# Attention with interleaved encoder work: stages handed out by a model of the engines' times, and the softmax sums' round trip through DRAM timed in microseconds

## The chip, the cores and the metric

The kernel runs on one core of a Trainium2 chip. The metric is device time in microseconds (us) for one execution; lower is better. The engines are TensorE (PE in the profile; PEld are its weight loads), VectorE (DVE), ScalarE (ACT), GpSimd (POOL) and SyncE (SP, which here only issues DMAs). Each takes its own instructions in the order in which the program was written.

## The reference

`x` has the shape (4, 1024, 256), that is B = 4 sequences of T = 1024 tokens with C = 256 channels. Two layers are added to it in turn.

```
def attn(x):                       # H = 16 heads of D = 16 channels
    q, k, v = split(x @ w_attn.T)
    att = q @ k.T / sqrt(16) + where(causal, slope[h] * (kpos - qpos), -inf)
    return (softmax(att) @ v) @ w_proj.T

def ffn(x):                        # attention over the 4 sequences, at each position
    q, k, v = split(x @ in_proj_w.T + in_proj_b)
    h = layernorm(x + softmax(q @ k.T / 4) @ v @ out_w.T + out_b)
    assign = max(top_2(softmax(h @ router_w.T + router_b)))   # one of 8 experts
    oe = gelu(h @ w1[assign].T + b1[assign]) @ w2[assign].T + b2[assign]
    return layernorm(h + oe)

x = x + attn(layernorm(x))
x = x + ffn(layernorm(x))
```

All of it is in float32. Attention is causal within a sequence of 1024 tokens. The second layer's attention mixes the four tokens that share a position, and each token then goes to one expert.

## The kernel before

**Attention.** The work is cut into 20 *units* (line 676 on). A unit is a batch `n`, that is a chunk `c` of 256 query tokens of a sequence `b`. In the last chunk the 256 tokens are split, so there are 8 units of 128 tokens (`size` 1); the others have `size` 2. For a unit and a group `g` of four heads, keys are taken in *rounds* of 512 columns: `score` (L951) makes the scores of a round on PE, 4 heads side by side in the rows, into two pairs of PSUM banks, ACT takes the exponentials, and `weigh` (L988) multiplies two rounds' results by the values. There are 160 rounds, that is 80 pairs `p`. `begins[u]` is the pair at which unit `u` starts; its last rounds are weighed one pair after its end.

The scores are transposed (keys on partitions), so the softmax sum of each query comes out as one more row of `yt`, next to 16 rows of each head. To divide, that row has to reach the partitions of its head. It goes through DRAM, all on SyncE's queue:

| step | what it issues |
| --- | --- |
| end of `weigh` | `y<-yt`: the unit's result to DRAM |
| `load_sums` (L1039) | `sums<-y`: the sums, spread over 128 partitions |
| `invert` (L1045) | DVE reciprocal, then `r<-inverse` to DRAM |
| `load_y` (L1053) | two times `su<-r` (each inverse repeated for 16 channels) and `yc<-y` |
| `divide` (L1070) | DVE: `yc` times `su` |
| `project` (L1079) | PE: `op<-wp,yc`; DVE adds it to `x` |

The last unit, 19, goes another way (`normalise`, `project_slots`).

**Preparing a batch.** For each `n` there are `x_norm` in three stages (L850), `turn` (L862), two `project_qk` (L875) and `value` (L897). `fill_slots` (L921) loads a group's queries and keys into `slots`, on SyncE, once the previous unit's last score of that group is out.

**Encoder fronts.** `front` (L1547) is a generator: the second layer's part ahead of the experts for 128 positions (512 tokens). It needs `x` after `project` of all four sequences. There are 8 fronts, 0 to 7. Front 7 is done after attention, with the first expert tiles; the others are spread through attention. At each `yield` a front says of which kind its next stage is, and its cost in us: "E" and "P" are work of DVE (P follows a result of another engine), "N" an exponential on ACT, "R" a power on POOL, "D" and "d" products on PE (d: a further one of the same kind), "DQ" the start of the projection to `qkv`, whose one buffer only one front can hold. A class `Running` keeps the next stage; at most two fronts are under way.

**Who decides the order.** Each pair `p` is written out as: `score_next(2p)`, `E_slot(2p)`, `D_slot(p)`, `fill()`, `take_E`, `score_next(2p+1)`, `weigh` of the two oldest rounds, `fill()`, `E_slot(2p+1)`. Steps with a fixed place are put in with `at_E(slot, ...)` and `at_D(pair, ...)`; the sums' steps stand at E slots `2e+3`, `2e+5`, `2e+6` and `2e+9` and at D slot `e+5`, with `e = begins[u+1]`, and the fronts of a chunk join the queue at E slot `2e+11`. The rest of a slot goes to the fronts: `take_E` (L2021) moves each front by at most one E, N, R or P stage, up to 2.5 us of cost in a slot (`E_SLOT`; 3.6 in the last chunk, `E_LATE`), and `take_D` (L2038) hands out D stages up to 5.6 us in a pair (`D_SLOT`), not in the slot in which the front's previous stage went out.

**After attention.** A second planner (L2293) places what is left of the fronts, front 7 and the expert tiles of the first six fronts; the remaining tiles follow when front 7's routing is known. An expert tile gathers 128 tokens of one expert (POOL), runs two products and a layer norm, and scatters its rows (POOL).

Of the kernel before, what the change touches and what calls it, by code (L numbers as in the profile page):

```python
# [37 lines left out]
P = 128  # L38
B, T, C = 4, 1024, 256
H, D, E = 16, 16, 8  # L40
S = 32
G = H // 4
# [5 lines left out]
PC = W // P  # L48
NC = T // W
# [20 lines left out]
TILE = (("PE", 2.6), ("DVE", 1.7), ("ACT", 1.9), ("POOL", 2.3))  # L70
TILE_HALF, LAG, COPIED, FIRST_BY, W1_THERE, LOAD_W2 = 1.3, 0.2, 1.0, 0.1, 22.0, 10.0
KQ_BUFS = 2
D_SLOT, E_SLOT, E_LATE = 5.6, 2.5, 3.6

EXP_ZERO = -126 * math.log(2.0)

# [526 lines left out]
def fast_layer(ctx: ExitStack, tc: tile.TileContext, odd, x, wq, wk, wv, wp, w_in, w_out, w_r,  # L603
# [32 lines left out]
    fact = ctx.enter_context(pool("fact", 1))  # L636
# [15 lines left out]

    half_of, n_pairs = [], [0]
    tail_banks = []

    def pair_of_banks(name):
        half_of.clear()
        n_pairs[0] += 1  # L660
        return ps_s.tile([P, 2, QC], F32, tag=f"s{n_pairs[0] % 4}", name=name)

    def bank(name):
# [9 lines left out]
    batches = [(c, b) for c in range(NC) for b in range(B)]  # L673


    units = [(n, 0, PC if n < (NC - 1) * B else 1) for n in range(NC * B)]
    units += [(n, i, 1) for i in range(1, PC) for n in range((NC - 1) * B, NC * B)]
    last_unit = len(units) - 1
# [23 lines left out]
    for j in range(4):  # L702
        r = j * S + D
# [99 lines left out]
    def norm_stats(src, n, name, tag=""):  # L803
        tiles = norm_tiles(name, tag)
        for i in range(n):
            norm_one(tiles, i, src(i))
        return norm_end(tiles, n)

    def norm_root(rstd, n):
        nc.gpsimd.tensor_tensor(  # L810
            rstd[:, :n], rstd[:, :n], minus_half.to_broadcast([P, n]), ALU.pow
        )
# [30 lines left out]
    sums, at = [], 0  # L843
# [6 lines left out]
    def x_norm(n, stage):  # L850
        c, b = batches[n]
        src = lambda i: xs[c, b][:, i]
        if stage == 0:
            held["norm", n] = norm_stats(src, PC, f"x_{n}", "_x")
        elif stage == 1:
            norm_root(held["norm", n][1], PC)
        else:
            xn = act.tile([P, PC, C], F32, tag="xn", name=f"xn_{n}")
            norm_apply(lambda i: xn[:, i], src, PC, *held.pop(("norm", n)), f"x_{n}")
            held["xn", n] = xn  # L860
# [76 lines left out]
    def blocks_of(u, r):  # L937

        n, i, size = units[u]
        first = batches[n][0] * PC + i  # L940
        some = QC // (size * P)
        return [
            (kb, max(0, kb - first) * P)
            for kb in range(some * r, min(some * (r + 1), first + size))
        ]

    def n_rounds(u):
        n, i, size = units[u]
        return -(-(batches[n][0] * PC + i + size) // (QC // (size * P)))
# [129 lines left out]
    def project(u):  # L1079
        yc, _ = held.pop(("y", u))  # L1080
        pm = bank(f"op_{u}")
        for i in range(units[u][2]):
            for cc in range(CC):
                nc.tensor.matmul(
                    pm[:, i * C:(i + 1) * C], yc[:, cc, i * P:(i + 1) * P], wp_sb[:, cc],
                    start=cc == 0, stop=cc == CC - 1,
                )
        add_attended(u, pm)
# [4 lines left out]
    for j in range(4):  # L1093
        at = slice(j * S, (j + 1) * S)
# [901 lines left out]

    class Running:
        def __init__(self, stages):
            self.stages, self.slot, self.was, self.ready = stages, -9, None, 0.0
            self.next()  # L2000

        def next(self):
# [2 lines left out]
                self.kind, self.cost, *self.more = self.kind  # L2005

    queue, running = [], []
    slot = [0]
    to_load, left_x = [], [0] * NC

    def load_next():
        while to_load and (
            to_load[0] < X_BUFS or left_x[(to_load[0] - X_BUFS) // B] == PC
        ):
            load_x(to_load.pop(0))

    def start_fronts():
        while queue and len(running) < 2:
            running.append(Running(queue.pop(0)))

    def take_E(cost=0.0, most=E_SLOT):  # L2021


        slot[0] += 1
        start_fronts()
        for it in list(running) if most > 0 else ():
            if it.kind in ("E", "N", "R", "P") and it.slot < slot[0] - (it.kind == "P"):
                of_it = it.cost if it.kind in ("E", "P") else 0.0
                if cost and cost + of_it > most:
                    continue  # L2030
                cost += of_it
                it.slot, it.was = slot[0], "E"
                it.next()
                if it.kind == "end":
                    running.remove(it)
        return cost

    def take_D(cost):  # L2038

        slot[0] += 1  # L2040
        for it in list(running):
            while it.kind[0] in "Dd":
                if it.kind == "DQ" and ("qkv",) in held:
                    break
                if it.kind != "d" or it.slot < slot[0]:
                    if it.slot >= slot[0] - (it.was == "E"):
                        break
                if cost and cost + it.cost > D_SLOT:
                    break
                if it.kind == "DQ":  # L2050
                    held["qkv",] = True
                cost += it.cost
                it.slot, it.was = slot[0], "D"
                it.next()
            if it.kind == "end":
                running.remove(it)
        return cost

    begins = [0]
    for u in range(len(units)):  # L2060
        begins.append(begins[-1] + G * n_rounds(u) // 2)
    of_E, of_D = {}, {}

    def at_E(k, what):
        of_E.setdefault(k, []).append(what)

    def at_D(k, cost, what):
        of_D.setdefault(k, []).append((cost, what))
# [4 lines left out]
    for u, (n, i, size) in enumerate(units):  # L2073
        c, b = batches[n]

        q = begins[u - 1] if u else -2
        e = begins[u + 1]
        if u == n:
            if n > 2:
                at_E(2 * begins[n - 3], lambda n=n: to_load.append(n))  # L2080
            for k in range(3):
                at_E(2 * q - 7 + k, lambda n=n, k=k: x_norm(n, k))
            at_D(q - 2, 0.9, lambda n=n: turn(n))

            at_D(q - (n == 0), 1.7, lambda n=n: project_qk(n, 0))
            at_D(q + (n > 0), 1.7, lambda n=n: project_qk(n, 1))
            at_D(q + 2, 1.7, lambda n=n: value(n))
        if u > 1:
            at_E(2 * q + 1, lambda u=u: load_values(u))
        if u < last_unit:  # L2090
            for at, what in ((3, load_sums), (5, invert), (6, load_y), (9, divide)):
                at_E(2 * e + at, lambda u=u, what=what: what(u))
            at_D(e + 5, 0.9 * size, lambda u=u: project(u))
        if b == B - 1 and u < last_unit:
            at_E(2 * e + 11, lambda c=c, i=i, size=size: queue.extend(
                front(PC * c + i + k, fact, 1, False) for k in range(size)
            ))
    at_E(2 * begins[last_unit] + 1, load_slotted)
    for g in range(2):
        at_D(begins[last_unit] + 2 + g, 0.5, lambda g=g: normalise(g))  # L2100
# [36 lines left out]

    fetching = [True]

    def E_slot(k, most=E_SLOT):  # L2140
        for what in of_E.pop(k, ()):
            what()
        load_next()
        if tables and fetching:
            experts.fetch()
        return take_E(0.0, most)

    def D_slot(p):
        todo = of_D.pop(p, ())
        for _, what in todo:  # L2150
            what()
        return take_D(sum(cost for cost, _ in todo))

    for p in range(-6, 0):
        E_slot(2 * p)
# [3 lines left out]
    rounds = [  # L2159
        (u, g, r) for u in range(len(units)) for g in range(G) for r in range(n_rounds(u))  # L2160
    ]
    waiting, to_fill = [], []

    def score_next(k):
        u, g, r = rounds[k]
        waiting.append((u, g, r, score(u, g, r)))
        if r == n_rounds(u) - 1 and u < last_unit:
            to_fill.append((u + 1, g))

    def fill():  # L2170
        while to_fill:
            fill_slots(*to_fill.pop(0))

    for p in range(len(rounds) // 2):
        most = E_SLOT if p < begins[(NC - 1) * B] else E_LATE

        then = most if p < len(rounds) // 2 - 1 else 0.0
        score_next(2 * p)
        E_slot(2 * p, most)
        D_slot(p)  # L2180
        fill()
        take_E(0.0, then)
        score_next(2 * p + 1)
        if len(waiting) > 2:
            weigh(waiting[:2])
            del waiting[:2]
        fill()
        E_slot(2 * p + 1, then)
    weigh(waiting)
    attention.close()  # L2190
    half_of.clear()
    tail_banks.append(ctx.enter_context(pool("ps_m", 3, space=PSUM)))


    for p in range(len(rounds) // 2, len(rounds) // 2 + 3):
        for k in (2 * p, 2 * p + 1):
            for what in of_E.pop(k, ()):
                what()
            if k % 2 == 0:
                for _, what in of_D.pop(p, ()):  # L2200
                    what()
    assert not of_E and not of_D, (sorted(of_E), sorted(of_D))
    for g in range(2, G):
        normalise(g)
    load_sums(last_unit)
# [87 lines left out]
    while threads:  # L2293
# [4 lines left out]
        at, _, it = min((begin(it) + FIRST_BY * n, n, it) for n, it in enumerate(threads))  # L2298
# [14 lines left out]
    n = 0  # L2313
# [98 lines left out]
```

## Time and profile before

| what | value |
| --- | --- |
| median of 3 runs | 840.61 us (839.70 to 841.50) |
| the profiled execution | 839.0 us; span of its instructions 837.3 us |
| granted clock of TensorE, mean | 0.945 |
| 38 to 107 us: first chunk, no fronts | PE busy 59.2 of 69 |
| 107 to 657 us: rest of attention with fronts 0 to 6 | PE 500.8, DVE 369.9, ACT 308.4 of 550 |
| 657 to 740 us: front 7 and tiles | PE 72.1, DVE 69.5 of 83 |
| 740 to 838 us: tiles | PE 67.2, POOL 69.3, DVE 59.1 of 98 |

The stretches come from a view of busy time by window. A line of the profile names an instruction by what it writes and reads, `yc<-yc,su` for the division. Nearly all instructions carry line 584, a helper that records every operation, so that names of tiles tell them apart. In a line of the timeline the numbers are start and length; a bracket holds the idle time of the engine just before, and what ended it. In a line of the waits they are total, number and longest.

### The profile page before, as it was taken

How to read it: one execution, taken by the hardware profiler on the slowest of the kernel's cores; microseconds unless marked ns; L12 is line 12 of the kernel's file. 1: busy time of each engine (PE TensorE's matmuls, PEld its weight loads, DVE VectorE, ACT ScalarE, POOL GpSimd, SP SyncE). 2: the span in 40 equal slices, each digit the busy share in tenths (PEclk: the TensorE clock that was granted, in tenths of full speed). 3: DMA queues.
4: the chain of work that ended last, by engine and by line, in shares of the span. 5: the costliest groups of instructions: out<-in, count | busy, mean ns of one | idle time of the engine just before them, and what ended most of it. 6: DMA issues, size and time to landing. Idle time of an engine off the chain costs nothing. (4 is left out here: it accounts for less than half of the span.)

```text
span 837.3 us, 22499 instructions
## 1 busy us (share of the span) xinstructions
PE 721.3 (86%) x8917; PEld 538.9 (64%) x8917; DVE 546.5 (65%) x1316; ACT 416.8 (50%) x625; POOL 254.3 (30%) x360
## 2 busy tenths in 40 slices
PE   3887879999899879999989996998988499878982
PEld 2665657666666556665667875766767368667772
DVE  7234326429647957595778758389389669885663
ACT  1454436656555736665455566466465145333540
POOL 5433113212111311121212212122121314648885
PEclk9899989999999989999989999999998899998996
DMA  7444445434522415252445534434431662233430
GB/s 214 117 127 137 133 142 143 137 111 125 158 80 76 119 50 170 56 162 71 128 117 145 148 105 149 120 87 131 131 90 29 192 230 76 69 108 120 124 103 24
DMA packets 75219, 99.56 MB, mean 119 GB/s; under 512 B 19496, under 2 KB 58723, under 8 KB 74596
## 3 DMA queue, kind: packets, MB, share of 16 engines
q1 hardware_dynamic: 64576, 79.63, 32.6%
q0 software_dynamic: 4864, 14.16, 5.7%
q10 hardware_dynamic: 5668, 4.25, 1.7%
q8 instruction: 73, 1.20, 0.6%
q14 instruction: 38, 0.31, 0.1%
HBM read 61.55 MB, written 35.12 MB: 115 GB/s over the span
## 5 line engine op out<-in xcount | busy, mean ns | idle before, releaser
L584 ACT ACTIVATE p<-sk 128x1024 f32<-128x1024 f32 (+1 forms) x320 | 288.2, 938 | 171.1 <-PE sk L584 147.0
L982 POOL TENSOR_SCALAR_AFFINE_SELECT p<-p 128x512 f32<-128x512 f32 (+1 forms) x160 | 105.3, 662 | 446.9 <-ACT p L584 444.5
L584 PE MATMUL sk<-slots 32*128 32x128 f32 (+1 forms) x3456 | 185.2, 334 | 17.2 <-ACT p L584 5.4
L584 PEld LDWEIGHTS sk<-slots 32*128 32x128 f32 x3456 | 139.5, 192 | 63.9 <-issue 23.0
L584 PE MATMUL pv<-p,v 128*32 128x128 f32 (+1 forms) x3456 | 146.7, 317 | 10.1 <-DVE kq L584 6.3
L584 PEld LDWEIGHTS pv<-p,v 128*32 128x32 f32 x3456 | 97.2, 112 | 48.9 <-issue 10.0
L584 PE MATMUL qkvp<-w_in,ut 128*128 128x264 f32 (+1 forms) x236 | 84.3, 491 | 0.0
L584 PEld LDWEIGHTS qkvp<-w_in,ut 128*128 128x128 f32 x236 | 41.7, 192 | 29.5 <-issue 25.2
L584 PE MATMUL oe<-w,ge 128*128 (+1 forms) x152 | 43.6, 411 | 12.8 <-DVE stats_v L584 6.9
L584 DVE COPY qkv<-qkvp 128x264 f32<-128x264 f32 x28 | 12.1, 432 | 63.0 <-PE qkvp L584 63.0
L584 PE MATMUL op<-wp,yc 128*128 128x256 f32 x124 | 34.5, 420 | 17.6 <-issue 6.2
L1809 POOL DMA_INDIRECT given<-rows,rows x38 | 42.6, 1120 | 21.5 <-DVE at_t L584 10.0
L584 PE MATMUL hid<-mt,w 128*128 128x128 f32 x304 | 46.0, 288 | 1.4 <-DMA w<-in_w_dram 0.8
L584 PEld LDWEIGHTS hid<-mt,w 128*128 128x128 f32 x304 | 41.2, 197 | 2.9 <-DMA w<-in_w_dram 1.0
L1925 POOL DMA_INDIRECT out_dram<-o,out_rows x38 | 39.5, 1039 | 8.7 <-issue 6.1
L584 DVE TENSOR_TENSOR pv<-qkv,sc 128x1024 f32<-128x1024 f32 x32 | 40.4, 1263 | 0.1
L584 PEld LDWEIGHTS op<-wp,yc 128*128 128x128 f32 x124 | 23.6, 203 | 25.2 <-issue 11.8
L584 DVE TENSOR_REDUCE sc<-pr 128x64 f32<-128x1024 f32 x32 | 39.0, 1220 | 1.1
L584 DVE TENSOR_TENSOR pr<-qkv 128x1024 f32<-128x1024 f32 x32 | 39.3, 1229 | 0.0
L584 ACT COPY qkv<-qkvp 128x512 f32<-128x512 f32 (+1 forms) x31 | 17.3, 561 | 43.1 <-PE qkvp L584 43.0
L584 PEld LDWEIGHTS oe<-w,ge 128*128 128x128 f32 x152 | 26.9, 198 | 17.4 <-DVE stats_v L584 7.3
L584 PE MATMUL qkp<-xt,wqk 128*128 128x256 f32 x144 | 37.7, 407 | 0.2 <-ACT p L584 0.2
(320 smaller groups left out, 1060.7 us busy)
## 6 DMA issues: line engine op xcount, KB each, us to landing
slots<-k SPq DMA_DIRECT2D x128, 80.0 KB
k<-kq SPq DMA_DIRECT2D x32, 256.0 KB
v<-v SPq DMA_DIRECT2D x16, 288.0 KB
v<-v SPq DMA_DIRECT2D x4, 1152.0 KB
x<-in_x_dram SPq DMA_DIRECT2D x16, 256.0 KB
y<-yt SPq DMA_DIRECT2D x16, 256.0 KB
rows<-x SPq DMA_DIRECT2D x32, 128.0 KB
slots<-k SPq DMA_DIRECT2D x64, 64.0 KB
```

What stands on the lines that cost most here:

```text
L584: ins = made(*args, **kwargs)
L982: nc.gpsimd.affine_select(blocks, blocks, pattern=[[0, 2], [0, size], [1, P]], compare_op=ALU.is_ge, fill=0.0, base=0, channel_multiplier=-1,)
L1809: nc.gpsimd.indirect_dma_start(out=self.hx, out_offset=None, in_=t.rows_of, in_offset=bass.IndirectOffsetOnAxis(ap=t.rows_[:, self.j:self. ...
L1925: ins = nc.gpsimd.indirect_dma_start(out=out.rearrange("t n c -> (t n) c"), out_offset=bass.IndirectOffsetOnAxis(ap=t.table.out_rows[:, t. ...
```

## The change

Budgets per slot are replaced by three clocks, `time["PE"]`, `time["DVE"]` and `time["ACT"]`, that run while the program is written out. Every score, weigh, product and DVE step adds its cost to its engine's clock, not before its input is ready; `pair_free` holds when each of the four pairs of PSUM banks comes free, and PE's clock waits for it. `take_E` hands out stages, more than one of a front if it can, as long as their input is ready by the clocks and DVE's clock is at most 1 us ahead of PE's. `take_D` asks for the same readiness, except for "d", and may fill 10 us of a pair. The sums' steps have due times counted from ACT's clock at the copy of the last `yt`, and go out at the first E slot (for `project`, the first D slot) at which PE's clock has passed them. The fronts of a chunk join the queue with the last `project`. Fixed places of the batches' own steps stay. The instructions, the tiles and their buffers stay as they are.

```diff
@@ -70,7 +70,10 @@
 TILE = (("PE", 2.6), ("DVE", 1.7), ("ACT", 1.9), ("POOL", 2.3))
 TILE_HALF, LAG, COPIED, FIRST_BY, W1_THERE, LOAD_W2 = 1.3, 0.2, 1.0, 0.1, 22.0, 10.0
 KQ_BUFS = 2
-D_SLOT, E_SLOT, E_LATE = 5.6, 2.5, 3.6
+D_SLOT = 10.0
+SWITCH, COLUMN, EXP_AT_ALL, EXP, READ = 0.2, 1 / 600, 0.17, 1 / 1200, 0.7
+AHEAD, EARLY_BY, ROOT, OF_D = 1.0, 0.2, 1.4, 0.35
+SUMS_BY, INVERTED_BY, Y_BY, DIVIDED_BY, PROJECTED_BY = 3.0, 6.5, 9.0, 13.0, 14.0
 
 EXP_ZERO = -126 * math.log(2.0)
 
@@ -652,12 +655,13 @@
 
 
 
-    half_of, n_pairs = [], [0]
+    half_of, n_pairs, taken = [], [0], []
     tail_banks = []
 
     def pair_of_banks(name):
         half_of.clear()
         n_pairs[0] += 1
+        taken.append(n_pairs[0] % 4)
         return ps_s.tile([P, 2, QC], F32, tag=f"s{n_pairs[0] % 4}", name=name)
 
     def bank(name):
@@ -1996,7 +2000,7 @@
 
     class Running:
         def __init__(self, stages):
-            self.stages, self.slot, self.was, self.ready = stages, -9, None, 0.0
+            self.stages, self.ready = stages, 0.0
             self.next()
 
         def next(self):
@@ -2005,7 +2009,6 @@
                 self.kind, self.cost, *self.more = self.kind
 
     queue, running = [], []
-    slot = [0]
     to_load, left_x = [], [0] * NC
 
     def load_next():
@@ -2014,55 +2017,83 @@
         ):
             load_x(to_load.pop(0))
 
+
+    time = {"PE": 0.0, "DVE": 0.0, "ACT": 0.0}
+    pair_free = [0.0] * 4
+
+    def busy(on, cost, ready=0.0):
+        time[on] = max(time[on], ready) + cost
+        return time[on]
+
+    def on_tensor(cost):
+        return busy("PE", cost, max([0.0] + [pair_free[k] for k in taken]))
+
+    def read_at(when):
+        for k in taken:
+            pair_free[k] = when
+        taken.clear()
+
+    def product(cost, what):
+        taken.clear()
+        what()
+        end = on_tensor(cost)
+        busy("DVE", OF_D * cost, end - 0.5 * cost)
+        read_at(max(end + READ, time["DVE"]))
+        return end
+
     def start_fronts():
         while queue and len(running) < 2:
             running.append(Running(queue.pop(0)))
 
-    def take_E(cost=0.0, most=E_SLOT):
-
-
-        slot[0] += 1
+    def take_E(some=True):
+
         start_fronts()
-        for it in list(running) if most > 0 else ():
-            if it.kind in ("E", "N", "R", "P") and it.slot < slot[0] - (it.kind == "P"):
-                of_it = it.cost if it.kind in ("E", "P") else 0.0
-                if cost and cost + of_it > most:
+        left = some
+        while left:
+            left = False
+            for it in list(running):
+                now, kind = time["PE"], it.kind
+                if kind not in ("E", "N", "R", "P"):
                     continue
-                cost += of_it
-                it.slot, it.was = slot[0], "E"
+                on = {"E": "DVE", "P": "DVE", "N": "ACT"}.get(kind)
+                if it.ready > max(now, time[on] if on else 0.0) + EARLY_BY:
+                    continue
+                if on == "DVE" and time["DVE"] > now + AHEAD:
+                    continue
+                if kind == "R":
+                    it.ready = max(now, it.ready) + ROOT
+                else:
+                    it.ready = busy(on, it.cost if on == "DVE" else 0.5, it.ready)
+                left = True
                 it.next()
                 if it.kind == "end":
                     running.remove(it)
-        return cost
 
     def take_D(cost):
 
-        slot[0] += 1
         for it in list(running):
             while it.kind[0] in "Dd":
                 if it.kind == "DQ" and ("qkv",) in held:
                     break
-                if it.kind != "d" or it.slot < slot[0]:
-                    if it.slot >= slot[0] - (it.was == "E"):
-                        break
+                if it.kind != "d" and it.ready > time["PE"] + EARLY_BY:
+                    break
                 if cost and cost + it.cost > D_SLOT:
                     break
                 if it.kind == "DQ":
                     held["qkv",] = True
                 cost += it.cost
-                it.slot, it.was = slot[0], "D"
-                it.next()
+                end = product(it.cost, it.next)
+                it.ready = max(end + READ, time["DVE"])
             if it.kind == "end":
                 running.remove(it)
-        return cost
 
     begins = [0]
     for u in range(len(units)):
         begins.append(begins[-1] + G * n_rounds(u) // 2)
     of_E, of_D = {}, {}
 
-    def at_E(k, what):
-        of_E.setdefault(k, []).append(what)
+    def at_E(k, what, cost=0.0):
+        of_E.setdefault(k, []).append((cost, what))
 
     def at_D(k, cost, what):
         of_D.setdefault(k, []).append((cost, what))
@@ -2079,7 +2110,7 @@
             if n > 2:
                 at_E(2 * begins[n - 3], lambda n=n: to_load.append(n))
             for k in range(3):
-                at_E(2 * q - 7 + k, lambda n=n, k=k: x_norm(n, k))
+                at_E(2 * q - 7 + k, lambda n=n, k=k: x_norm(n, k), (1.0, 0.0, 0.8)[k])
             at_D(q - 2, 0.9, lambda n=n: turn(n))
 
             at_D(q - (n == 0), 1.7, lambda n=n: project_qk(n, 0))
@@ -2087,14 +2118,34 @@
             at_D(q + 2, 1.7, lambda n=n: value(n))
         if u > 1:
             at_E(2 * q + 1, lambda u=u: load_values(u))
-        if u < last_unit:
-            for at, what in ((3, load_sums), (5, invert), (6, load_y), (9, divide)):
-                at_E(2 * e + at, lambda u=u, what=what: what(u))
-            at_D(e + 5, 0.9 * size, lambda u=u: project(u))
-        if b == B - 1 and u < last_unit:
-            at_E(2 * e + 11, lambda c=c, i=i, size=size: queue.extend(
-                front(PC * c + i + k, fact, 1, False) for k in range(size)
-            ))
+
+
+    due_E, due_D = [], []
+
+    def attended(u, at):
+        size = units[u][2]
+        if u == last_unit:
+            return
+        for by, what, cost in (
+            (SUMS_BY, load_sums, 0.0), (INVERTED_BY, invert, 0.3), (Y_BY, load_y, 0.0),
+            (DIVIDED_BY, divide, 0.5),
+        ):
+            due_E.append((at + by, cost, lambda what=what: what(u)))
+        due_D.append((at + PROJECTED_BY, 0.9 * size, lambda: projected(u)))
+
+    def projected(u):
+        n, i, size = units[u]
+        c, b = batches[n]
+        project(u)
+        if b == B - 1:
+            queue.extend(front(PC * c + i + k, fact, 1, False) for k in range(size))
+
+    def pop_due(due, now):
+        some = sorted((it for it in due if it[0] <= now), key=lambda it: it[0])
+        for it in some:
+            due.remove(it)
+        return [(cost, what) for _, cost, what in some]
+
     at_E(2 * begins[last_unit] + 1, load_slotted)
     for g in range(2):
         at_D(begins[last_unit] + 2 + g, 0.5, lambda g=g: normalise(g))
@@ -2137,19 +2188,20 @@
 
     fetching = [True]
 
-    def E_slot(k, most=E_SLOT):
-        for what in of_E.pop(k, ()):
+    def E_slot(k, some=True):
+        for cost, what in of_E.pop(k, []) + pop_due(due_E, time["PE"]):
             what()
+            busy("DVE", cost)
         load_next()
         if tables and fetching:
             experts.fetch()
-        return take_E(0.0, most)
+        take_E(some)
 
     def D_slot(p):
-        todo = of_D.pop(p, ())
-        for _, what in todo:
-            what()
-        return take_D(sum(cost for cost, _ in todo))
+        todo = of_D.pop(p, []) + pop_due(due_D, time["PE"])
+        for cost, what in todo:
+            product(cost, what)
+        take_D(sum(cost for cost, _ in todo))
 
     for p in range(-6, 0):
         E_slot(2 * p)
@@ -2161,45 +2213,56 @@
     ]
     waiting, to_fill = [], []
 
+    def columns_of(u, r):
+        return sum(units[u][2] * P - off for _, off in blocks_of(u, r))
+
     def score_next(k):
         u, g, r = rounds[k]
+        taken.clear()
         waiting.append((u, g, r, score(u, g, r)))
+        end, n = on_tensor(SWITCH + columns_of(u, r) * COLUMN), columns_of(u, r)
+        for pair in list(taken):
+            pair_free[pair] = busy("ACT", EXP_AT_ALL + 2 * n * EXP, end)
         if r == n_rounds(u) - 1 and u < last_unit:
             to_fill.append((u + 1, g))
+
+    def weigh_next(some):
+        taken.clear()
+        weigh(some)
+        end = on_tensor(SWITCH + sum(columns_of(u, r) for u, _, r, _ in some) * COLUMN)
+        read_at(busy("ACT", 0.4, end))
+        u, g, r, _ = some[-1]
+        if g == G - 1 and r == n_rounds(u) - 1:
+            attended(u, time["ACT"])
 
     def fill():
         while to_fill:
             fill_slots(*to_fill.pop(0))
 
     for p in range(len(rounds) // 2):
-        most = E_SLOT if p < begins[(NC - 1) * B] else E_LATE
-
-        then = most if p < len(rounds) // 2 - 1 else 0.0
+        then = p < len(rounds) // 2 - 1
         score_next(2 * p)
-        E_slot(2 * p, most)
+        E_slot(2 * p)
         D_slot(p)
         fill()
-        take_E(0.0, then)
+        take_E(then)
         score_next(2 * p + 1)
         if len(waiting) > 2:
-            weigh(waiting[:2])
+            weigh_next(waiting[:2])
             del waiting[:2]
         fill()
         E_slot(2 * p + 1, then)
-    weigh(waiting)
+    weigh_next(waiting)
     attention.close()
     half_of.clear()
     tail_banks.append(ctx.enter_context(pool("ps_m", 3, space=PSUM)))
 
 
-    for p in range(len(rounds) // 2, len(rounds) // 2 + 3):
-        for k in (2 * p, 2 * p + 1):
-            for what in of_E.pop(k, ()):
-                what()
-            if k % 2 == 0:
-                for _, what in of_D.pop(p, ()):
-                    what()
     assert not of_E and not of_D, (sorted(of_E), sorted(of_D))
+    for _, what in pop_due(due_E + [], 1e9) + pop_due(due_D + [], 1e9):
+        what()
+    for it in running:
+        it.ready = 0.0
     for g in range(2, G):
         normalise(g)
     load_sums(last_unit)
```

## The prediction

> **What bounds the kernel now.** I read the page's header first, then busy time by stretch, then who waited for whom on TensorE and VectorE, then SyncE's queue in order of time.
>
> ```profile
> span 837.3 us, 22499 instructions
> PE 721.3 (86%) x8917; PEld 538.9 (64%) x8917; DVE 546.5 (65%) x1316; ACT 416.8 (50%) x625; POOL 254.3 (30%) x360
> ```
>
> ```profile
> 107.00:657.00 550.00, 500.79 (x7291) 362.18 (x7292) 369.85 (x817) 308.37 (x415) 112.62 (x156) 0.97 0.40 115
> 657.00:740.00 83.00, 72.08 (x405) 57.67 (x404) 69.46 (x183) 33.58 (x71) 32.42 (x34) 0.90 0.45 144
> 740.00:838.00 98.00, 67.19 (x468) 57.90 (x467) 59.12 (x182) 32.00 (x71) 69.31 (x99) 0.89 0.30 92
> ```
>
> Columns: stretch, length, busy PE, PEld, DVE, ACT, POOL. From 107 us (attention with encoder work mixed in) to 657 PE works 501 of 550 us: it sets the pace, in program order. From 657 to 740 (last front, first expert tiles) PE (72 of 83) and DVE (69) share the limit. After 740 the tiles alone run. So in the long stretch only PE's idle 49 us can be won; moving PE work inside it wins nothing. This is what PE waited for between 100 and 657:
>
> ```profile
> PE ctp L584 <- DVE ctx L584: 7.7, 5, 2.0
> PE op L584 <- issue: 6.2, 4, 5.0
> PE xtp L584 <- DVE xn L584: 6.1, 4, 5.6
> PE op L584 <- ACT p L584: 5.1, 3, 2.0
> ...
> PE qkp L584 <- DVE ctx L584: 2.7, 2, 2.0
> ...
> PE op L584 <- DVE yc L584: 2.1, 1, 2.1
> ```
>
> Late results of DVE are most of it: `ctx`, `xn` and the divided `yc`. DVE itself waited for the way of the sums through DRAM (38 to 657 us), nearly all in its first units:
>
> ```profile
> DVE inverse L584 <- DMA sums<-y: 16.2, 5, 7.3
> ...
> DVE yc L584 <- DMA yc<-y: 8.3, 4, 4.0
> ```
>
> One such way, SyncE's queue and then DVE:
>
> ```profile
> 153.37 0.37 SPq L1049 DMA_DIRECT2D r<-inverse  x1
> 155.10 0.66 SPq L1064 DMA_DIRECT2D su<-r  x1
> 155.81 0.59 SPq L1067 DMA_DIRECT2D yc<-y  x1
> 156.45 0.57 SPq L1064 DMA_DIRECT2D su<-r  x1
> 157.07 0.57 SPq L1067 DMA_DIRECT2D yc<-y  x1
> ```
>
> ```profile
> 161.30 0.69 DVE L584 TENSOR_TENSOR yc<-yc,su 128x512 f32<-128x512 f32 x1 [0.76 <-DMA yc<-y]
> ```
>
> The division waited, so its start is the landing: 161.30 - 155.10 = **6.2 us** from the first of the four loads (6.0 and 6.6 at 101.11 and 135.52, two other divisions that waited). `r` to `su` is 1.7 us. `sums<-y` at 121.96 let `inverse` start at 124.31 after a wait: 2.35 us.
>
> **What the Trainium skill says.** "Perfetto Trace Analysis", section DMA Instruction - HWDGE (DVE, Sync): the profiler's span of such a DMA ends when the sequencer is free; the movement is not in it. The trace agrees: 0.57 us of issue for the last load, data 3.7 us after it. "DMA: Bandwidth & Descriptors", section Anatomy of one DMA: about 2 us of a DMA are fixed, mostly the receipt of the last write (fitted there for GpSimd's path); here 1.7 to 2.4 us for small SyncE transfers, in line. "TensorE: Matmul & The Clock Gate", section Step-by-step: matmuls stay in program order, only weight loads are pulled ahead. The table above fits: a late `yc` holds scores that need nothing of it.
>
> **Part 1, the model instead of budgets.** No instruction is added or removed; stages move. Before, a front got at most one E stage per call under 2.5 or 3.6 us, whether DVE was late or not. Now a stage goes out when the model has its input ready (`EARLY_BY` 0.2) and DVE is at most 1 us ahead of PE. Waits for inputs that the model knows should mostly go: ctp 7.7 and qkp 2.7 are gone, **-10**. Of xtp's 6.1 (`x_norm` keeps its fixed slot, but stands behind less backlog) half, **-3**. GpSimd's `norm_root` (1.0 us) and select (0.66) move along; POOL is busy 113 of 550, so nothing. ACT keeps its exps; 308 of 550 covers it. If that cover failed, scores would wait for banks: D may now take 10 us per pair of rounds, an ACT lull behind PE work, so nothing.
>
> Fronts get faster. One front's E and P costs sum to 38 us of DVE, evictions to 0.35 x 20.6 = 7: 45 us. The fronts ended at 263, 329, 414, 483, 562, 624 and 693 us (reduction of `rank`), 70 us apart; at 45 plus 5 us per unit they need about 55. Front 6 now begins near 555 and ends before 657. In the tail before it had from 661 to 694 about 20 us of DVE (two weighted sums 4.7, evictions 2.4, statistics 2.5, keys and ranks 6, `u` by G1 and B1 2.5, counts 1.4) and 7 us of PE (8 `ctp`, 12 `ao`, 1 `place`). Both engines being near the limit there, I take half the DVE time from the tail, **-10**, and put PE's 7 us into attention, **+7**. Bounds for both together: -13 (tail loses all 20) to +7.
>
> **Part 2, sums' way by time.** Per unit the same DMAs on SyncE: `sums<-y`, `r<-inverse`, two `su<-r`, two `yc<-y`. Before, load_sums, invert, load_y, divide, project stood at E slots 3, 5, 6, 9 and D slot e+5: 1.5 pairs of rounds, at 7 to 9 us each, between load_y and divide. Now they become due at 3.0, 6.5, 9.0, 13.0 and 14.0 us of modelled time after the last `yt`. What was 37 us is 14; a load gets 4 us to land where the trace says 6.2; and due steps are only looked up at E slots.
>
> Those slots come in couples: one at the end of a pair of rounds (c), one after the next score (b), about 1 us on (0.2 + 512/600 = 1.05; 1.17 in the trace), then D, a score and a weigh (1.05 + 1.91) to the next c. With a weigh ending at 0, `at` is about 0.5. b is at 1.05; first c at 4.0 + D1; b 1.05 on; next c at 8.0 + D1 + D2; b 9.05 + D1 + D2. Over a unit D1 holds project_qk 1.7, D2 value and turn 2.6, plus what fronts give (X). Due: sums 3.5, inverse 7.0, y 9.5, divide 13.5, project 14.5.
> - X = 0: sums at c 5.7; inverse **and** y at c 12.3; divide next c (16.3); project at b 17.3, 5 us after the inverse. Needed: 0.35 + 0.4 + 1.7 + 6.2 + 0.7 = 9.4. PE waits about 4.
> - X = 2.5 in D1: sums and inverse at c 8.2; y **and** divide at c 14.8; project at b 15.8. Needed 6.9, there is 1.2: PE waits over 5.
> - X = 8 in D1: the first three at c 13.7, divide too or at the next slot; project two couples on at best: 3 to 4.
>
> Where divide stands right behind its loads, DVE stands still for 5 us, with evictions of `qkv`, `kq` and `x` behind it; SyncE sits on `su<-r` with the key loads of `slots` behind. These waits lie inside PE's, so I don't add them.
>
> Units 3 to 10: 8 x 5 = 40. Units 11 to 14, mostly loads of half the size: 4 x 4 = 16. Units 15 to 18, fewer D's: 4 x 1. First three units: 8 pairs take 69 us (38 to 107), 8.6 each against 6.6 modelled, so nothing. Sum 60. A PE that stood finds exps done and banks free, and catches up with DVE; I count a quarter back: **+45** (bounds +10, if slots drift apart, to +75). The old waits of op for yc go: **-8** (6.2 + 2.1).
>
> **Sum:** -10 -3 -10 +7 +45 -8 = +21 us. The profiled execution took 839.0 us (span 837.3 plus 1.7), so 860; it stands 1.6 under the median 840.6, so **861**.
>
> **Rivals.**
> - Faster. Model time runs slower than real time (score 1.05 modelled, 1.17 real, and model waits add), so steps fall into slots further apart and the loads land: part 2 then costs +10 instead of +45, 839 + 21 - 35 = 825, 827 on the median's scale; with the tail's full 20 us, 817. For: old DVE waits for these loads nearly vanished after the first units. Against: then there were 11 us in between.
> - Slower still. DVE's stall delays `kq` and the key loads, so the next unit's scores wait for slots too. Before: PE pv stood 5.0 us behind `kq`, itself behind a 7.3 us wait for sums. If half of 16 units do this for 4 us: +32, 893. It decides once a stall ends after the last D before a unit's change.
> - It does nothing: stages keep pace because DVE's order is bound by evictions anyway (`qkv` waited 63 us for PE), and stalls old and new are alike: 839 to 842.
>
> **Chances.** Forecast (845 to 880) 0.57, faster 0.29, slower still 0.10, nothing 0.04. Below 826 and above 888 I leave some 0.18. About 0.2%, 1.7 us, is what a measurement here can tell from no change: faster 0.29, same 0.04, slower 0.67. The likeliest case's own range is 845 to 880.
>
> **What would show it.** Right: PE op waiting for DVE yc for 30 us and more, DVE yc for DMA beyond 50; `ctp` behind `ctx` near 0; fronts some 55 us apart, front 6's `place` before the first `mtp`; 107 us to the end of attention longer than 550, the tail shorter. Wrong: op's waits under 15 us in all with an end of attention at or before 657 (then the slots leave time enough); or front 6 still in the tail.

## The result and the profile after

| | before | after |
| --- | --- | --- |
| median | 840.15 us (4 runs) | 917.04 us (4 runs, 913.43 to 919.38) |
| ratio, 95% interval | | 1.0918, 1.0868 to 1.0968 |
| profiled execution, span | 839.0, 837.3 us | 919.4, 917.7 us |
| last `y<-yt` of attention issued at | 656.0 us | 729.1 us |

The change makes the kernel 9.2% slower. The forecast was slower at 861; the loss is 77 us where I had 21. The header of the changed kernel's page, then its busy time by stretch (stretch, length, busy PE, PEld, DVE, ACT, POOL with the number of instructions in brackets, then PE's clock, the share of the DMA engines and GB/s):

```profile
span 917.7 us, 22503 instructions
PE 736.4 (80%) x8917; PEld 550.0 (60%) x8917; DVE 545.4 (59%) x1316; ACT 416.7 (45%) x625; POOL 251.9 (27%) x360
```

```profile
107.00:729.00 622.00, 524.65 (x7395) 379.33 (x7395) 366.19 (x814) 314.94 (x425) 107.69 (x154) 0.92 0.35 101
729.00:813.00 84.00, 68.45 (x369) 54.74 (x370) 65.88 (x165) 31.47 (x68) 36.35 (x37) 0.90 0.44 147
813.00:918.00 105.00, 72.24 (x505) 62.93 (x504) 65.43 (x203) 34.41 (x77) 69.17 (x99) 0.87 0.29 91
```

PE's instructions are the same 8917, yet PE is busy 15 us longer, and from 38 us to the end of attention it idles 118 us (691 less 573) where it idled 59 (619 less 560). So of the 80 us between the two spans, 59 are new idle time of PE in attention, 13 are longer matmul time there (for 20 matmuls fewer), and 8 lie after it. Who PE waited for, 100 to 729 us (total, number, longest):

```profile
PE op L587 <- DVE yc L587: 31.2, 4, 9.3
PE qkp L587 <- DVE yc L587: 17.7, 2, 12.9
PE sk L587 <- issue: 11.0, 1, 11.0
PE passed L587 <- DVE yc L587: 7.2, 1, 7.2
...
PE sk L587 <- DVE rank L587: 5.2, 2, 3.7
```

The tile behind `project` takes other names when it shares its pair with another product (`qkp`, `passed`, `xtp`): all four lines with `DVE yc` are one wait, 63.7 us from 38 us on. DVE in turn, 38 to 729 us:

```profile
DVE yc L587 <- DMA yc<-y: 116.5, 18, 14.5
DVE qkv L587 <- PE qkvp L587: 47.3, 23, 4.1
DVE inverse L587 <- DMA sums<-y: 45.6, 12, 7.4
```

Before, the first was 8.3, the second 63.0 and the third 16.2. One such place in order of time, SyncE, DVE and PE together:

```profile
119.30 1.72 SPq L939 DMA_DIRECT2D slots<-k  x4
121.11 0.37 SPq L923 DMA_DIRECT2D v<-v  x1
121.53 0.65 SPq L1068 DMA_DIRECT2D su<-r  x1
...
123.48 0.57 SPq L1071 DMA_DIRECT2D yc<-y  x1
128.43 0.69 DVE L587 TENSOR_TENSOR yc<-yc,su 128x512 f32<-128x512 f32 x1 [14.53 <-DMA yc<-y]
129.04 0.68 DVE L587 COPY kq<-qkp 128x512 f32<-128x512 f32 x1
129.82 1.77 PE L587 MATMUL sk<-slots 32*128 32x256 f32 x12 [10.97 <-issue]
```

DVE came to the division at 113.9 (128.43 less 14.53). SyncE sent the first of its loads at 121.53, behind key loads (`slots<-k`) in its queue that had themselves stood 5.3 us for the keys' way to DRAM (`k<-kq`), and the data took 6.9 us. All that time `kq` could not be copied out of PSUM; it was copied right after the division, and PE's scores, which have nothing to do with `yc`, went on 0.1 us after that copy. They had stood for 11 us. At 9 of the 19 divisions DVE came before the first load was even sent; that part is 39 of the 116 us, and the rest lies behind the first load's issue. (The eight `y<-yt` of the first chunk go out on ACT's queue; all else on the sums' way is on SyncE's.)

### The profile page after: what moved, and what is told of

It is laid out like the page before. It is cut to its first block, busy times and chain, and to the rows that moved or that the text cites. A ratio compares the mean times of both kernels' runs of the same rounds, so it can differ in the third digit from the quotient of the medians.

```text
span 917.7 us, 22503 instructions
## 1 busy us (share of the span) xinstructions
PE 736.4 (80%) x8917; PEld 550.0 (60%) x8917; DVE 545.4 (59%) x1316; ACT 416.7 (45%) x625; POOL 251.9 (27%) x360
## 5 line engine op out<-in xcount | busy, mean ns | idle before, releaser
L587 PE MATMUL pv<-p,v 128*32 128x128 f32 (+1 forms) x3456 | 151.4, 324 | 8.4 <-ACT p L587 6.5
L587 PEld LDWEIGHTS pv<-p,v 128*32 128x32 f32 x3456 | 100.6, 114 | 48.6 <-issue 14.5
L587 DVE TENSOR_TENSOR yc<-yc,su 128x512 f32<-128x512 f32 (+1 forms) x19 | 11.4, 598 | 116.5 <-DMA yc<-y 116.5
L587 PE MATMUL qkvp<-w_in,ut 128*128 128x264 f32 (+1 forms) x224 | 76.5, 477 | 0.0
L587 PEld LDWEIGHTS qkvp<-w_in,ut 128*128 128x128 f32 x224 | 39.6, 190 | 27.0 <-issue 22.3
L587 PE MATMUL op<-wp,yc 128*128 128x256 f32 x60 | 21.2, 500 | 42.0 <-DVE yc L587 31.2
L587 PE MATMUL qkp<-xt,wqk 128*128 128x256 f32 x208 | 51.7, 392 | 0.2 <-ACT p L587 0.2
L587 PE MATMUL hid<-mt,w 128*128 128x128 f32 x304 | 48.5, 298 | 3.5 <-DMA w<-in_w_dram 3.1
L587 PEld LDWEIGHTS qkp<-xt,wqk 128*128 128x128 f32 x208 | 37.5, 189 | 9.7 <-issue 3.0
L587 PEld LDWEIGHTS op<-wp,yc 128*128 128x128 f32 x60 | 13.5, 243 | 46.4 <-issue 32.2
```

The lines of the kernel that those rows point to most:

```text
L587: ins = made(*args, **kwargs)
```

## The experiments

The theory after the first look (S): the sums' steps come too close, so the in-order DVE stands at the division and at the inverse. The rival (M): the pacing by the model, with lumps of 10 us of D, is what loses. Times are medians, ratios against before in the same group of runs (835.2, 835.4 and 834.7 us; the change itself was measured against 840.2, so its loss is 77 us).

**e1: the sums back at fixed slots, the model kept**

```diff
-        if g == G - 1 and r == n_rounds(u) - 1:
-            attended(u, time["ACT"])
+            for at, what, cost in ((3, load_sums, 0.0), (5, invert, 0.3), (6, load_y, 0.0), (9, divide, 0.5)):
+                at_E(2 * e + at, lambda u=u, what=what: what(u), cost)
+            at_D(e + 5, 0.9 * size, lambda u=u: project(u))      # fronts at 2 * e + 11
```

> The changed kernel with the sums' steps put back at the fixed slots of before (E slots 2e+3, 5, 6, 9, D slot e+5, fronts at 2e+11); clocks, take_E, take_D and D_SLOT 10 stay. Theory S (all of the loss lies in the sums' way): back to 825 to 845 us, DVE's wait for yc's loads under 15 us. Rival M (the pacing by the model, with D stages in lumps of up to 10 us, loses): 880 to 920 us, only a part comes back.

848.5 us, 1.0166 (1.0123 to 1.0208). So the sums' way makes nearly all of the loss, and the model alone still loses 13 us, which S had not expected; DVE still waits 22.5 us for `yc`, where S had under 15. The place of the 13 is not where M puts it. Busy time by stretch, attention in the change and then e1:

```profile
38.00:729.00 691.00, 572.82 (x7879) 415.14 (x7878) 393.15 (x883) 340.12 (x467) 127.36 (x188) 0.91 0.36 103
```

```profile
38.00:635.00 597.00, 548.97 (x7883) 400.99 (x7875) 379.47 (x847) 340.50 (x469) 132.99 (x190) 0.98 0.43 120
635.00:659.00 24.00, 8.10 (x49) 5.47 (x50) 18.89 (x54) 3.56 (x7) 4.34 (x4) 0.63 0.52 174
```

With the same pacing and practically the same matmuls, attention takes 691 us with the sums by time and 597 with the sums by slots. The price of the sums' way is thus some 94 us there, in the profiled executions (e1's is 5 us under its median): 70 of idle time of PE (118 against 48) and 24 of longer matmul time.

Attention in e1 ends at 635 us, 21 before the old kernel's 656. But then PE works 8 of 24 us, until the first expert tile at 658.8. The tile needs the first *table* (the list of the tokens that a tile gathers), and the table needs the last step of front 5 (the *place* of each token within its expert), which comes at 621 us, 13 before the end of attention; before, it came at 624 with 32 us of attention still to go. What attention won, the stretch behind it loses.

**e2: the budgets of before, the sums by time**

```diff
-D_SLOT = 10.0                    # and take_E, take_D by the clocks
+D_SLOT = 5.6                     # take_E, take_D as before the change; the clocks only time the sums
```

> The other half alone: fronts handed out by the budgets of before (2.5 and 3.6 us per slot, D 5.6), the clocks only kept to time the sums' steps at 3.0, 6.5, 9.0, 13.0 and 14.0 us. Theory S: as slow as the whole change, 900 to 925 us, with DVE waiting some 100 us for yc's loads. Rival M: near before, 840 to 860 us.

983.0 us, 1.1766 (1.1724 to 1.1807): beyond both. DVE waits 136 us for `yc` and 47 for the sums. The due times alone cost 148 us on the old pacing; in the whole change, which loses 77, the model takes back some 71 of them.

**e4: divide and project 14 us later**

```diff
-SUMS_BY, INVERTED_BY, Y_BY, DIVIDED_BY, PROJECTED_BY = 3.0, 6.5, 9.0, 13.0, 14.0
+SUMS_BY, INVERTED_BY, Y_BY, DIVIDED_BY, PROJECTED_BY = 3.0, 6.5, 9.0, 27.0, 28.0
```

> The changed kernel with divide and project due 14 us later (27.0 and 28.0 instead of 13.0 and 14.0); sums, inverse and load_y as in the change. Theory S with the division as the place: DVE's wait for yc's loads falls from 116 us to under 20, time 835 to 855 us; the 46 us that DVE waits for sums stay and cost PE at most 10. Rival: the sums' wait at the inverse matters as much, then 870 to 890.

845.0 us, 1.0105 (1.0049 to 1.0162). DVE's wait for `yc` does not appear any more; two numbers take back some 67 of the 77 us, as S has it. DVE's wait for the sums did not stay at 46 us: it is 73.

**e6: only project later**

```diff
+SUMS_BY, INVERTED_BY, Y_BY, DIVIDED_BY, PROJECTED_BY = 3.0, 6.5, 9.0, 13.0, 28.0
```

> The changed kernel with only project due later (28.0 instead of 14.0); divide stays at 13.0, so DVE still stands in the division for its loads, but no matmul needs yc soon. If PE's own wait for yc is the loss (my prediction): 845 to 860 us. If a DVE that stands in the division holds PE through the evictions behind it (kq, qkv, yt): DVE's wait stays near 110 us and the time at 880 to 905 us, with PE waiting for kq, qkv or banks instead of yc.

926.1 us, 1.1076 (1.1041 to 1.1111): in all nothing comes back, it is a little slower than the change, and beyond both ranges. DVE's waits of e6, and PE's, from 38 us to 720:

```profile
DVE yc L587 <- DMA yc<-y: 111.8, 17, 13.9
```

```profile
PE sk L587 <- issue: 13.2, 1, 13.2
PE pv L587 <- DVE kq L587: 12.8, 3, 7.4
PE sk L587 <- DVE kq L587: 12.8, 4, 9.8
PE ctp L587 <- DVE ctx L587: 9.8, 4, 5.3
```

No matmul waits for `yc` now, and PE still idles 106 us up to the end of attention at 717 (118 up to 729 in the change), mostly for whatever DVE has behind the division: `kq`, `ctx`, and further down `ct`, `ut` and `u`. So 12 us of attention came back of the 64 that PE had waited for `yc`, and they were lost again behind attention (207 us against 189; why, see the table under e8 to e11). My prediction had PE's own wait for `yc` as the price. It is for the most part only the form that the price took in that order of the program.

**e7: the inverse and the loads later too**

```diff
+SUMS_BY, INVERTED_BY, Y_BY, DIVIDED_BY, PROJECTED_BY = 3.0, 12.0, 14.0, 27.0, 28.0
```

> The changed kernel with the inverse and load_y later too: 3.0, 12.0, 14.0, 27.0, 28.0. In e4 DVE still stood 73 us at the inverse. If that wait costs PE: 10 to 20 us under e4 (825 to 835). If what is left over of the loss is the tail's wait for fronts (theory F), no change against e4 within 5 us, because the fronts still get only some 13 of front 6's 31 stages handed out before attention ends.

828.9 us, 0.9895 (0.9852 to 0.9938): **far faster than the change, and 1% under the kernel before**, a small gain. DVE waits 17.6 us for sums (73.4 in e4) and 7.6 for `yc`. So the waits at the inverse, priced at 10 us at most in e4's text, cost about 16 us there (e7 also moves `load_y`, so that this is not the inverse alone; e13 below is); theory F, by which nothing would change, was wrong on this point.

**e8, e9, e10, e11: DVE further ahead**

```diff
-AHEAD, EARLY_BY, ROOT, OF_D = 1.0, 0.2, 1.4, 0.35
+AHEAD, EARLY_BY, ROOT, OF_D = 2.0, 1.0, 1.4, 0.35     # e8: on e1; e11: on e7
+AHEAD, EARLY_BY, ROOT, OF_D = 3.0, 2.0, 1.4, 0.35     # e9: on e1; e10: on e7
```

> e1 (sums at the fixed slots) with DVE allowed 2 us ahead of PE and EARLY_BY 1.0 instead of 1.0 and 0.2. As written out, front 6 then has more stages before the end of attention and front 5's table is made there. Theory F (e1 loses in the tail, which waits for front 6 and the first table): attention longer than in e1's 622 us but the first expert tile sooner, total 815 to 832 us. Rival (DVE's backlog then delays evictions and attention loses what the tail wins): 835 to 850.

> The same with 3 us ahead and EARLY_BY 2.0. Theory F: 810 to 830 us, first expert tile at about 645 us or before. Rival (backlog): 840 to 860, with PE waiting for ctx, kq and qkv again.

> e7's due times with 3 us ahead and EARLY_BY 2.0: the change with both of its faults mended as I understand them. Theory F: within 8 us of e9, 810 to 830 us. Rival (backlog): as for e9, 840 to 860.

> e7's due times (3.0, 12.0, 14.0, 27.0, 28.0) with 2 us ahead and EARLY_BY 1.0. e8 against e1 won 15 us, e9 nothing. If the two mendings add, 815 to 825 us; if attention's loss and the tail's gain cancel here, as e7 has the fronts far enough on already, 827 to 838.

| kernel | median | ratio (95%) | last `y<-yt` | first tile | rest after attention |
| --- | --- | --- | --- | --- | --- |
| before | 835 to 840 | 1 | 656 | 661 | 181 |
| after | 917 | 1.0918 (1.0868 to 1.0968) | 729 | 734 | 189 |
| e1 | 848 | 1.0166 (1.0123 to 1.0208) | 635 | 659 | 206 |
| e8 | 833 | 0.9972 (0.9953 to 0.9991) | 644 | 649 | 188 |
| e9 | 849 | 1.0086 (1.0048 to 1.0124) | 664 | 680 | 179 |
| e7 | 829 | 0.9895 (0.9852 to 0.9938) | 620 | 643 | 206 |
| e11 | 833 | 0.9972 (0.9947 to 0.9998) | 639 | 643 | 192 |
| e10 | 845 | 1.0102 (1.0079 to 1.0125) | 660 | 665 | 182 |

The last columns are times in the profiled execution and its span less the last `y<-yt`. (The 622 us in the expectation of e8 is e1's last `y<-yt` but one; its attention ends at 635.) As DVE may run further ahead, attention gets longer and the rest shorter. The first step, to 2 us, makes attention 9 us longer and the rest 18 shorter on e1, and 18 and 14 on e7: the medians fall by 16 us and rise by some 5. The second, to 3 us, costs 20 and 21 us of attention for 9 and 10 of the rest. So encoder work is for the most part moved across the end of attention, not hidden. Theory F missed its range three times (e8 by 1 us); at 3 us it is the rival's case, though PE's waits for `ctx`, `kq` and `qkv` grew only in part: in e9 PE waits 12.7 us for banks at `op`, 7.6 for `xn` and 12.0 for `kq`.

The length of the rest goes with the first table. In e1, e4, e6 and e7 front 5's place came 11 to 14 us before the end of attention; the first tile's gather then came 18 to 20 us after that end, and the rest took 200 to 207 us. In the nine other kernels front 5's place came 25 us or more before the end and the gather before it, and the rest took 179 to 193.

**e12 and e13: the kernel before, one number each**

```diff
-            for at, what in ((3, load_sums), (5, invert), (6, load_y), (9, divide)):
+            for at, what in ((3, load_sums), (5, invert), (6, load_y), (6, divide)):     # e12
+            for at, what in ((3, load_sums), (3, invert), (6, load_y), (9, divide)):     # e13
```

> The kernel before with one number changed: divide at E slot 2e+6, where load_y stands, instead of 2e+9; project stays where it was, some 2 pairs of rounds later. If a DVE that waits in the division holds PE up through its other work (the reading of e6): DVE's wait for yc's loads near 100 us, and 875 to 910 us. If the wait itself costs nothing: 835 to 845.

> The kernel before with invert at E slot 2e+3, where load_sums stands, instead of 2e+5. DVE then waits for every sums<-y, some 2.3 us at least and more where SyncE is behind: 45 to 80 us in all. If such waits cost PE as in e4 against e7 (16 us for 56 us of DVE's waits): 845 to 858 us. If they hide: within 5 us of before.

e12: 966.5 us, 1.1563 (1.1517 to 1.1609). e13: 881.1 us, 1.0545 (1.0506 to 1.0585). Both beyond the range I gave. DVE's wait in e12, and in e13:

```profile
DVE yc L584 <- DMA yc<-y: 174.4, 19, 13.6
```

```profile
DVE inverse L584 <- DMA sums<-y: 97.9, 18, 13.1
```

What PE waited for in e12, 38 to 790 us, the two longest lines; none is for `yc`:

```profile
PE sk L584 <- DVE kq L584: 26.4, 7, 13.8
PE ctp L584 <- DVE ctx L584: 25.4, 5, 10.8
```

In neither does a matmul need the result soon: in e12 `project` is where it was. One number in the untouched kernel makes a loss larger than the whole change. DVE's waits for the two DMAs together against the time, over the span of each profiled run: before 24.5 us (839), e7 25 (828), e1 43 (843), e4 73 (844), e13 98 (884), e6 150 (926), after 162 (919), e12 181 (971), e2 183 (981). Against before in their own groups, the medians of the kernels from e13 on pay 0.56 to 0.93 us for each further us in which DVE stands; between e7 and e4 it is 0.33.

## Why the prediction went wrong

**The mechanism's first half was right.** The steps clump as worked out: a load needs 6.2 us (5.7 to 6.9 at the first four divisions after), DVE comes to the division less than 4 us behind its first load at 15 of 19, and 18 of 19 divisions wait. PE's direct waits for `yc`, 63.7 us, look like the 60 of the sum by units, but that is luck. The sum had 0, 40, 16 and 4 us for units 0 to 2, 3 to 10, 11 to 14 and 15 to 18; the trace has 18, 15, 24 and 7. The "so nothing" for the first three units was wrong: DVE stood 8.1, 11.8 and 14.5 us at their divisions.

**The step that failed first** is the term "**+45**", and in it "A PE that stood finds exps done and banks free, and catches up with DVE; I count a quarter back". The change against e1, which differs in the sums' way alone (and with it in when the fronts join the queue), gives what this term had to be: 94 us of attention. Of these 70 are idle time, more than all direct waits for `yc`, so no quarter came back; and 24 are longer matmul time, for which the prediction had no term. How matmuls get longer, see the last section.

**The second** is "These waits lie inside PE's, so I don't add them", of DVE's standing and SyncE's late key loads. Waits for things behind the division stand beside those for `yc`: 11.0 for the scores above and 3.7 of the 5.2 for `rank`. e6 and e12 show that I had the order of causes the wrong way round: the division holds DVE, and PE pays at the first thing it needs of DVE, `yc` or not. The rival "Slower still" came nearest with 893, at a chance of 0.10 too low. Its first half, `kq` delayed by DVE's stall, is what the scores above show; of its second, scores that wait for `slots`, PE's waits in attention show nothing. Its price was still short.

**The third** is the tail, "-10" and "+7", bounded by -13 to +7. The tail became 8 us longer. Front 6 was still in it, one of the signs that the prediction had named for being wrong. The fronts did not get faster: their places came at 280, 357, 425, 512, 637, 693 and 800 us, 87 apart in the mean against 72. Front 6, which I had ending before attention, was placed 71 us after its end (37 before). I took the 45 us of DVE cost for what limits a front. DVE is not that full: from 107 us on it works 370 of 550 before and 366 of 622 after. A front alternates between PE and DVE, and DVE stands in order for PE's products too (`qkv` 63 us before, 47 after). That a front's pace is set by how its stages lie between the rounds is my reading; no run shows it. In e1, where DVE's waits for DMAs are small again, the mean is 76.

**What held:** the waits that the model knows. PE stood 10.4 us behind `ctx` in two lines and 6.1 behind `xn`; after, `ctp` waits 1.3 for `ctx`, `op` 1.3 and `xtp` less than 1 for `xn`. In e1, where PE hardly stands for the sums, it is 1.2 for `ctx` and 1.5 for `xn` too, so that this is the model and not a PE that comes late. The terms -10 and -3 were sized about right. The -8 was not the model's: `op`'s 6.2 of issue is 0.5 after, but 5.7 in e1. e1's attention is 21 us shorter than before, 11 of idle time and 10 of matmul time (at a granted clock of 0.98 against 0.96).

**The rival "Faster"** needed the slots to drift apart far enough in real time for the loads to land. They did not: at 9 of 19 divisions DVE came before its loads were sent, most of them behind key loads in SyncE's queue, and at 6 more less than 4 us after.

What stays open: why the waits at the inverse were 73 us in e4 and 46 in the change, with the same due times for the sums and the inverse; and what the change would have cost with the loads on another queue than SyncE's, where no key loads stand ahead of them. No run tells.

## What to carry to other kernels

On an engine that works in order, an instruction that waits for a DMA costs what stands behind it, so its distance from the DMA has to be counted from where the load's queue really issues it, and a due time in a planner has to include the queue's own delay and the granularity of the slots at which it is looked up. Test it by moving the consumer of the waiting instruction away: if the time stays, as in e6, the waiting engine is the cause. A stage that is sped up (here attention, by 21 us in e1) gives the gain back where the next one waits for a slower chain (front 5 and the first table), so look at what the next stage waits for first.

## What the runs showed of the hardware that I had not expected

PE is slower for a while after it has stood. The 8 matmuls of `project` in the changed kernel, without a wait, and then 6 of them after one:

```profile
137.28 1.97 PE L587 MATMUL router<-wp,yc 128*128 128x256 f32 x8
```

```profile
489.45 2.90 PE L587 MATMUL op<-wp,yc 128*128 128x256 f32 x6 [8.78 <-DVE yc L587]
```

That is 0.25 against 0.48 us each. Busy time over these two places (all 8 matmuls of the second take 3.75 us):

```profile
137.28:139.25 1.97, 1.97 (x14) 1.48 (x13) 0.43 (x3) 0.00 (x0) 0.00 (x0) 1.00 0.02 7
489.45:493.21 3.76, 3.76 (x12) 2.55 (x12) 2.15 (x9) 0.00 (x0) 1.01 (x1) 0.50 0.01 2
```

The granted clock was 1.00 over the first and 0.50 over the second. Of the 19 times that `project` ran in the change, all eight after a wait of 4.8 us or more had a clock of 0.50 to 0.57; of the six after 1.4 to 3.2 us five had 1.00. The same shows over whole runs: PE's busy time is 711 us in e7, 721 before, 736 after, 747 in e2 and 749 in e12, for the same 8917 matmuls, while the mean granted clock falls from 0.949 (e7) over 0.908 (after) to 0.884 (e12). The Trainium skill, "TensorE: Matmul & The Clock Gate", section What's actually happening, has a gate that halves the clock after about 3.4 us of idling; the ratio of two and the eight longer waits fit it. I had counted a stall as something of which PE wins a part back, and it costs extra.
